# Two-engine halves for four PSUM copies, and a new pace for the background work, in a convolution, attention and mixture-of-experts kernel

## The chip, the core and the metric

The kernel runs on one core of one Trainium2 chip. A core has TensorE (PE in the profile; its weight loads are PEld), VectorE (DVE), ScalarE (ACT), GpSimd (POOL) and SyncE (SP, which here only issues DMAs). The metric is device time of the whole program in microseconds (us); lower is better. All data are float32.

## The reference, cut to what matters

```python
x = conv_attention(x)                 # (2, 256, 56, 56): 8 groups, linear attention, folded to one 256x256 map, + x, relu
t = to_tokens(x)                      # (2, 3136, 256)
n = layer_norm(t)
q, k, v = split(n @ W_attn)           # 4 heads of 64
t = t + softmax(causal(q k^T / 8)) v @ W_proj
n = layer_norm(t)
top2 of softmax(n @ gate_w + gate_b)  # 8 experts
t = t + sum over the two of weight * (gelu(n @ W1[e] + b1[e]) @ W2[e] + b2[e])
```

## The kernel before

**Stages.** In the profiled execution the convolution layer fills the first 94 us, attention of the two batches runs from 94 to about 865 us, and the experts with the sums at the end take the rest. The change touches `layer1`, which holds attention and experts.

**Attention.** A batch has 3136 tokens in 25 tiles of 128. Queries go in seven segments (`i` from 0 to 6) of W = 448 columns, heads in two pairs (`hp`). For each (i, hp), `attend` walks over the key tiles up to the diagonal: one *step* per key tile j. A step is `scores` (eight TensorE instructions of L660 into PSUM, then exp on ScalarE, L668; on the diagonal the causal mask on VectorE, L670; then the running sum of the exponentials on VectorE, L682, or L678 for the first) and, three steps later, `values` (L700). Key tiles that the diagonal cuts are interleaved with whole ones. Score tiles have two PSUM buffers (`psc`), exponentials five SBUF buffers.

**Visits.** When the steps of an (i, hp) are issued, `visit(i, hp)` is called, and then `sum_rows`, four small matmuls (`sp`, L724) of the running sum, copied out by ScalarE (L729). A visit prepares the next segment with *pieces* from `project_qkv`: at hp = 0 four Q/K projections (`query_key`, L540, copied out at L548), at hp = 1 one V projection for each of the next segment's token tiles (`value`, L557, copied out at L566, then L577 on VectorE), and at both a group of transposes of normalised rows (`transpose`, L526, copied to `px` at L532; GpSimd normalises, L511). The segments that are projected are 512 wide, the last two 384 and 192 (four V tiles, then three, then two). At i = 6 of the first batch the pieces are those of the second batch's first segments; at i = 6 of the second there are none. Each piece writes one PSUM bank of the pool `pm`, which has **two** buffers; products of the background, row sums, gate and sorting matmuls use the same two.

**Background work.** Generators stand in `queue`. `pull(n)` takes n items from them: a generator yields True after a piece of work, False when it can't go on, and "pe" when its next work is a matmul group; then it is *held* until `products()` in a visit lets it run (or a pull with `every`, in the experts' stage). `tokens(b)` runs in order: `project_gate` (batch 0; wt, wg), `project_out` (for pairs of tiles: matmuls `pp` L610, VectorE addition L615, then variances with `stats`, L168 and L169), `dispatch` (some 80 small VectorE operations that compute softmax, top two and slots, in `op`, `small_piece` and `apart` pauses; then 25 rows, each normalised on VectorE at L1294 and written by two indirect DMAs of GpSimd at L1302), the loads of w1 (SyncE) and the first expert rows. Batch 0's list runs during batch 1's attention, batch 1's in the experts' stage, where `meanwhile` pulls two or three items with `every` for each block of 128 rows. `between` is called before each step: on every second step it pulls two items. `visit` pulls twice as well.

**Order.** Attention and experts stand under a manual schedule: each engine executes in the order in which the program issues. An instruction that waits holds up all that stands behind it on its engine.

The lines around which the change turns:

```python
def visit(i, hp):
    now, then = ahead(b, i, hp)
    for piece in now:
        piece()
    for _ in range(2):
        pull()
        products()
    for piece in then:
        piece()
```

Of the kernel before, what the change touches and what calls it, by code (L numbers as in the profile page):

```python
# [28 lines left out]
def conv_attn_moe_kernel(  # L29
# [419 lines left out]
    def layer1(nm, general):  # L449

        with ExitStack() as whole:
# [45 lines left out]
            def project_qkv(b, qT, kT, v, px):  # L497

                def tiles(s):
                    return s[0] // P, -(-s[1] // P)  # L500

                todo = deque(p for s in SEGS for p in pairs(*tiles(s)))
                ready = {}

                def normalise():
                    if not todo:
                        return
                    n, m, k = todo.popleft()
                    xn = bg.tile([P, 2, C], F32, tag="xn", name=f"xn_{nm}{b}_{n}")
                    for a in range(m):  # L510
                        nc.gpsimd.tensor_scalar(  # L511
                            xn[:k, a], ts[b][:k, n + a, :C],
                            ts[b][:k, n + a, MEAN : MEAN + 1], ts[b][:k, n + a, RSTD : RSTD + 1],
                            ALU.subtract, ALU.mult,
                        )
                    ready[n] = xn

                def transpose(s, n, m, k):
                    if not ready:
                        normalise()  # L520
                    xn = ready.pop(n)
                    normalise()
                    tp = bank(f"xp_{b}_{n}", (P, NH, 2 * P))
                    for a in range(m):
                        for c in range(NH):
                            nc.tensor.transpose(  # L526
                                tp[:, c, a * P : a * P + k],
                                xn[:k, a, c * P : (c + 1) * P],
                                ident[:k, :k],
                            )  # L530
                    o, wp = n * P - SEGS[s][0], (m - 1) * P + k
                    nc.scalar.copy(px[:, s % 2, :, o : o + wp], tp[:, :, :wp])  # L532

                def query_key(s, which, hp):
                    first, end = SEGS[s]
                    w = end - first
                    ps = bank(f"qk_{b}_{s}_{which}_{hp}")
                    d0 = which * C + hp * P
                    for c in range(NH):
                        nc.tensor.matmul(  # L540
                            ps[:, :w],
                            wat[:, c, d0 : d0 + P],
                            px[:, s % 2, c, :w],
                            start=(c == 0),
                            stop=(c == NH - 1),
                        )
                    to = kT[hp] if which else qT[:, hp]
                    nc.scalar.copy(to[:, first:end], ps[:, :w])  # L548

                def value(s, n):  # L550
                    if b == 0 and n == 0:
                        centre_gate()
                    k = chunk(n)
                    ps = bank(f"v_{b}_{n}", (P, 512))
                    o = n * P - SEGS[s][0]
                    for c in range(NH):
                        nc.tensor.matmul(  # L557
                            ps[:k, : C + E],
                            px[:, s % 2, c, o : o + k],
                            wv[:, c].rearrange("p h d -> p (h d)"),  # L560
                            start=(c == 0),
                            stop=(c == NH - 1),
                        )
                    half = (C + E) // NH
                    for hp in range(NH):
                        nc.scalar.copy(  # L566
                            v[hp][:k, n].rearrange("p a d -> p (a d)"),
                            ps[:k, hp * half : (hp + 1) * half],
                        )
                    first, end = tiles(SEGS[s])  # L570
                    if n + 1 < end:
                        return
                    full = [n for n in range(first, end) if chunk(n) == P]
                    for f, e, k in ((first, first + len(full), P), (first + len(full), end, chunk(end - 1))):
                        for hp in range(NH if f < e else 0):
                            c0 = C + 2 * hp * LH
                            nc.vector.tensor_tensor(  # L577
                                ts[b][:k, f:e, c0 : c0 + 2 * LH].rearrange("p n (a e) -> p n a e", a=2),
                                v[hp][:k, f:e, :, HS:],
                                ts[b][:k, f:e, SLOT : SLOT + 1].unsqueeze(3).to_broadcast(  # L580
                                    [k, e - f, 2, LH]
                                ),
                                ALU.mult,
                            )
                    read[b] = end == NCH

                def xs(s):
                    return [partial(transpose, s, *p) for p in pairs(*tiles(SEGS[s]))] if s < NS else []

                def qks(s):  # L590
                    return [partial(query_key, s, which, hp) for which in range(2) for hp in range(NH)]

                def vs(s):
                    return [partial(value, s, n) for n in range(*tiles(SEGS[s]))]

                return xs, qks, vs
# [3 lines left out]
            def project_out(b, qT, done):  # L600

                for first, m, k in pairs():
# [3 lines left out]
                    for n in range(first, first + m):  # L606
# [8 lines left out]
                        nc.vector.tensor_tensor(t, t, ps[:k, : C + E], ALU.add)  # L615
                        if b == 0:
                            nc.sync.dma_start(out=rest_d[:k, n], in_=t[:, :C])
                    stats(b, first, m, k, bg, f"o{nm}{b}")

                    for _ in range(3 if b else 1):  # L620
                        yield True

            def attend(
                b, qT, kT, v, fst, fs, psc, py, visit, between, clock, later, finished
# [145 lines left out]
                for n in range(len(steps) + LAG):  # L770
# [3 lines left out]
                        sum_rows(hp, i)  # L774
                    if n < len(steps):
                        i = steps[n][0]
                        between(i, ends[i] - n)

                    late = n >= LAG and steps[n - LAG][3]
                    if n >= LAG:  # L780
# [162 lines left out]
            def dispatch(b):  # L943

                t = ts[b]
                tail = chunk(NCH - 1)
                ops = [0]

                def small_piece():

# [7 lines left out]

                def op():

                    ops[0] += 1
                    for _ in range(0 if b else 1 + ops[0] % 2):
                        yield True

                def small(name, last=E, dt=F32):
# [2 lines left out]
                def wide(ap):  # L968
# [8 lines left out]
                    small(k, 1).rearrange("p t o -> p (t o)") for k in ("newton_x", "newton_y", "red")  # L977
                )
                nc.vector.tensor_scalar(x, var, 1e-5, None, ALU.add)
                nc.vector.tensor_scalar(  # L980
                    y.bitcast(I32), x.bitcast(I32), 1, None, ALU.arith_shift_right
                )
                nc.vector.tensor_scalar(
                    y.bitcast(I32), y.bitcast(I32), -1.0, float(0x5F3759DF), ALU.mult, ALU.add
                )
                yield from small_piece()
                for i in range(4):
                    to = var if i == 3 else y
                    nc.vector.tensor_tensor(z, y, y, ALU.mult)
                    nc.vector.tensor_tensor(z, z, x, ALU.mult)  # L990
                    nc.vector.tensor_scalar(z, z, -0.5, 1.5, ALU.mult, ALU.add)
                    nc.vector.tensor_tensor(to, y, z, ALU.mult)
                    yield from op()
                    yield from small_piece()
# [294 lines left out]
                for n in range(NCH):  # L1289
# [23 lines left out]
                        if b or k:  # L1313
                            yield True
                    if b == 0:
                        yield False
                sent[b] = True

            def experts(w1s, w2s, b2s, ex, es, ps6, between, need, written):
# [327 lines left out]
            def pull(n=1, every=False):  # L1647

                while n > 0:
                    for g in list(queue):  # L1650
                        if g in held and not every:
                            continue
                        r = advance(g)
                        while r == "pe" and every:
                            r = advance(g)
                        if r is None or r is True:
                            n -= r is True
                            break
                    else:
                        return  # L1660
# [89 lines left out]
            else:  # L1750
# [26 lines left out]
                for b in range(B):  # L1777
                    queue.append(tokens(b, qT, lambda b=b: min(finished[b])))

                    def visit(i, hp):  # L1780

                        now, then = ahead(b, i, hp)
                        for piece in now:
                            piece()
                        for _ in range(2):
                            pull()
                            products()
                        for piece in then:
                            piece()

                    def between(i, left):
                        if b == B - 1 and i == NB - 1:

                            now = load_w2(left < NCH - 4)
# [1 line left out]
                                next(now, None)  # L1796

                        tick[0] += 1
                        if tick[0] % 2:
                            pull(2)  # L1800

                    due = attend(
                        b, qT, kT, v, fst, fs, psc, py, visit, between,
# [237 lines left out]
```

## Time and profile before

| | us |
|---|---|
| median of 16 runs (1297.36 to 1302.03) | 1299.76 |
| the profiled execution | 1300.63 |
| its span, first to last instruction | 1298.9 |
| TensorE busy in the span | 1251.7 |
| VectorE busy | 791.6 |
| ScalarE busy | 610.6 |
| mean granted TensorE clock | 0.993 |

A line of the timeline has the start (us from the span's start), the length of a run of like instructions, engine, line, operation, written tile and read tiles, the shape, the count, and in brackets the engine's idle time just before it with what ended it. A line of the waits has the waiting instruction, what released it, the total in us, how often, and the longest. Running instructions can overlap on TensorE, so that a run's length may reach past the start of the next.

### The profile page before, as it was taken

The page shows a single profiled execution, that of the slowest core. Times are in us where ns is not written, and L with a number is a line of the kernel's source. Part 1 is how long each engine was busy: PE and PEld are TensorE (multiplying, and loading weights), DVE is VectorE, ACT ScalarE, POOL GpSimd, SP SyncE. Part 2 cuts the span into 40 slices and gives each one's busy share as a digit, 9 for nine tenths or more (in the row PEclk, how much of TensorE's full clock was granted, in tenths as well). Part 3 has the DMA queues.
Part 4 walks back from the last instruction along what each step waited for, and adds up shares of the span by engine and source line. Part 5 has one row for each costly group of instructions (what it writes and reads, how often), then busy time and mean ns, then how long its engine had stood idle before and what let it go on. Part 6 is the DMA issues. An engine that isn't in the chain of part 4 may idle for free.

```text
span 1298.9 us, 28049 instructions
## 1 busy us (share of the span) xinstructions
PE 1251.7 (96%) x10569; PEld 821.9 (63%) x10569; DVE 791.6 (61%) x1659; ACT 610.6 (47%) x1228; POOL 350.9 (27%) x317
## 2 busy tenths in 40 slices
PE   7998999999999999999999999999999999999994
PEld 7874445444444454534444444469899899989993
DVE  1482557676677764668687877755675443455552
ACT  0144555465656555356555655552433333444441
POOL 1102412110002204221115760000047312675641
PEclk9999999999999999999999999999999999999997
DMA  9995011000000000100001243231135443576553
GB/s 294 383 304 179 16 24 33 25 9 25 9 17 9 26 1 11 39 9 16 9 9 61 93 162 103 71 100 53 54 126 169 127 114 95 153 226 204 180 162 103
DMA packets 110655, 123.55 MB, mean 95 GB/s; under 512 B 20019, under 2 KB 100260, under 8 KB 110512
## 3 DMA queue, kind: packets, MB, share of 16 engines
q1 hardware_dynamic: 97104, 93.12, 23.9%
q0 software_dynamic: 9984, 25.76, 5.9%
q10 hardware_dynamic: 3424, 2.78, 0.7%
q8 instruction: 87, 1.43, 0.5%
q14 instruction: 56, 0.46, 0.1%
HBM read 62.65 MB, written 60.41 MB: 95 GB/s over the span
## 4 chain that ended last, share of the span: by engine, by line
PE 79%; DVE 6%; DMA 5%; issue 4%; ACT 2%; POOL 2%; POOLq 0%; DVEq 0%; ACTq 0%; SPq 0%
PE yp_f L700 17%; PE sc_f L660 16%; PE ht_f L1421 13%; PE yp_f L1440 12%; PE qk_f L540 6%; PE cp L330 3%; PE v_f L557 3%; DVE acc_f L682 3%; PE gram L261 2%; PE pp_f L610 2%; POOL x_slots L1302 2%; ACT st_f L668 2%; PE tp_f L1398 2%; DMA y_tokens<-ys_f,to_f 1%; DMA kept<-t 1%
## 5 line engine op out<-in xcount | busy, mean ns | idle before, releaser
L668 ACT ACTIVATE st_f<-sc_f 128x896 f32<-128x896 f32 (+5 forms) x400 | 331.0, 840 | 215.1 <-PE sc_f L660 197.7
L682 DVE TENSOR_TENSOR acc_f<-acc_f,st_f 128x896 f32<-128x896 f32 (+5 forms) x372 | 379.6, 1020 | 67.6 <-ACT st_f L668 56.3
L700 PE MATMUL yp_f<-st_f,v_f 64*64 64x448 f32 (+6 forms) x3184 | 339.8, 501 | 4.6 <-DVE st_f L670 3.5
L660 PE MATMUL sc_f<-qT_f,kT_f 64*64 64x448 f32 (+6 forms) x3184 | 339.7, 499 | 3.3 <-ACT st_f L668 2.1
L1430 ACT ACTIVATE g_f<-ht_f,b1b 128x128 f32<-128x128 f32 x408 | 116.3, 368 | 222.6 <-PE ht_f L1421 222.5
L660 PEld LDWEIGHTS sc_f<-qT_f,kT_f 64*64 64x64 f32 x3184 | 122.5, 133 | 154.3 <-issue 124.7
L700 PEld LDWEIGHTS yp_f<-st_f,v_f 64*64 64x64 f32 x3184 | 119.8, 133 | 155.6 <-issue 131.3
L1421 PE MATMUL ht_f<-xT_f,w_f 128*128 128x128 f32 x1632 | 199.4, 275 | 0.8 <-ACT xT_f L1402 0.8
L1421 PEld LDWEIGHTS ht_f<-xT_f,w_f 128*128 128x128 f32 x1632 | 196.1, 192 | 5.6 <-ACT xT_f L1402 1.0
L712 POOL TENSOR_TENSOR qT_f<-both_f 128x448 f32<-128x448 f32 x28 | 37.0, 1322 | 488.7 <-ACT both_f L711 488.6
L1302 POOL DMA_INDIRECT x_slots<-xr_f,idx x100 | 111.8, 1118 | 127.7 <-DVE xr_f L1300 90.6
L511 POOL TENSOR_SCALAR xn_f<-t 128x256 f32<-128x256 f32 (+1 forms) x50 | 80.2, 1611 | 172.0 <-PE xp_f L526 66.2
L1409 DVE COPY w_f<-w1s_f 128x1024 f32 x102 | 71.1, 698 | 54.4 <-PE ht_f L1421 52.8
L1457 POOL DMA_INDIRECT y_tokens<-ys_f,to_f x60 | 61.8, 1030 | 121.8 <-DVE ys_f L1450 96.4
L1450 DVE TENSOR_TENSOR ys_f<-yp_f,kT_f 128x128 f32<-128x128 f32 x102 | 29.6, 290 | 101.9 <-PE yp_f L1440 97.5
L540 PE MATMUL qk_f<-px_f,wat 128*128 128x512 f32 (+2 forms) x224 | 88.1, 546 | 1.2 <-ACT px_f L532 1.2
L540 PEld LDWEIGHTS qk_f<-px_f,wat 128*128 128x128 f32 x224 | 40.6, 190 | 46.9 <-issue 41.6
L670 DVE TENSOR_TENSOR st_f<-st_f,keep 128x256 f32<-128x256 f32 (+1 forms) x112 | 45.4, 405 | 32.8 <-ACT st_f L668 32.8
L678 DVE COPY acc_f<-st_f 128x896 f32<-128x896 f32 x28 | 17.7, 633 | 77.1 <-ACT st_f L668 76.8
L1440 PE MATMUL yp_f<-px_f,g_f 128*128 x204 | 61.4, 383 | 0.0
L1440 PE MATMUL yp_f<-v_f,g_f 128*128 x204 | 61.1, 382 | 0.0
L1440 PE MATMUL yp_f<-kT_f,g_f 128*128 x204 | 61.1, 382 | 0.0
(255 smaller groups left out, 1254.3 us busy)
## 6 DMA issues: line engine op xcount, KB each, us to landing
x_slots<-fill SPq DMA_DIRECT2D x1, 8127.0 KB
xb_f<-x_slots SPq DMA_DIRECT2D x60, 129.0 KB
x_slots<-fill SPq DMA_DIRECT2D x1, 7296.0 KB
y_slots<-ys_f SPq DMA_DIRECT2D x57, 128.0 KB
kept<-t SPq DMA_DIRECT2D x2, 3200.0 KB
x<-in_x_dram SPq DMA_DIRECT2D x14, 448.0 KB
rb_f<-inverses SPq DMA_DIRECT2D x56, 112.0 KB
xr<-in_x_rows_dram SPq DMA_DIRECT2D x12, 512.0 KB
```

The source lines that it names most:

```text
L511: nc.gpsimd.tensor_scalar(xn[:k, a], ts[b][:k, n + a, :C], ts[b][:k, n + a, MEAN : MEAN + 1], ts[b][:k, n + a, RSTD : RSTD + 1], ALU.subtr ...
L540: nc.tensor.matmul(ps[:, :w], wat[:, c, d0 : d0 + P], px[:, s % 2, c, :w], start=(c == 0), stop=(c == NH - 1),)
L660: nc.tensor.matmul(ps[h : h + HS, a, c0:W], kT[hp][rows, j * P + h : j * P + h + HS], qT[rows, hp, q0 + c0 : q0 + W], start=True, stop=True,)
L668: nc.scalar.activation(st[:k, :, c0:], ps[:k, :, c0:W], AF.Exp, scale=SCALE)
L682: nc.vector.tensor_tensor(acc[:k, :, c0:], acc[:k, :, c0:], st[:k, :, c0:], ALU.add)
L700: nc.tensor.matmul(yp[a * HS : (a + 1) * HS, h // HS, c0:W], v[hp][h : h + HS, j, a, :HS], st[h : h + HS, a, c0:], start=first, stop=bool( ...
L1302: s = nc.gpsimd.indirect_dma_start(out=xds[b], out_offset=bass.IndirectOffsetOnAxis(ap=idxs[b][:kk, k, n : n + 1], axis=0), in_=xr[:kk], i ...
L1409: nc.vector.tensor_copy(w, w1s[:, :, bass.ds(e, 1), :].rearrange("p c e h -> p c (e h)"))
L1421: nc.tensor.matmul(ht[:, k, :], w[:, c, k * P : (k + 1) * P], xT[:, c, :], start=(c == 0), stop=(c == NH - 1),)
L1430: nc.scalar.activation(g[:, k, :], ht[:, k, :], AF.Gelu, bias=b1bs[b][:, k, i : i + 1])
L1440: nc.tensor.matmul(yp[:, :C], g[:, k, :], w2s[k][:, bass.ds(e, 1), :].rearrange("p e d -> p (e d)"), start=(k == 0), stop=(k == KH - 1),)
L1457: s = nc.gpsimd.indirect_dma_start(out=y_tokens, out_offset=bass.IndirectOffsetOnAxis(ap=to[:, n % GB : n % GB + 1], axis=0), in_=ys, in_o ...
```

## The change

Four parts:

- `leave` copies a projection's result out of PSUM in two halves: the first by ScalarE, the second by VectorE. Transposed rows are halved by the two row groups of 128 channels, Q and K by columns, V by head pair. Until now ScalarE made the whole copy (for V, two copies).
- A visit issues all its pieces, transposes included, and then the background's products. It pulls nothing any more.
- The variances of projected tiles become generators of their own (`closer`), put at the front of the queue, one tile an item. `dispatch` gives up one operation an item in batch 0, the Newton steps included; a scattered row takes two items.
- `between` pulls one item at every step, but none at the cut steps of the first segment. A pull with `every` lets a generator go past at most one "pe" and counts the next one as an item.

```diff
--- before.py
+++ after.py
@@ -499,6 +499,11 @@
                 def tiles(s):
                     return s[0] // P, -(-s[1] // P)
 
+                def leave(first, second):
+
+                    nc.scalar.copy(*first)
+                    nc.vector.tensor_copy(*second)
+
                 todo = deque(p for s in SEGS for p in pairs(*tiles(s)))
                 ready = {}
 
@@ -529,7 +534,7 @@
                                 ident[:k, :k],
                             )
                     o, wp = n * P - SEGS[s][0], (m - 1) * P + k
-                    nc.scalar.copy(px[:, s % 2, :, o : o + wp], tp[:, :, :wp])
+                    leave(*((px[:, s % 2, c, o : o + wp], tp[:, c, :wp]) for c in range(NH)))
 
                 def query_key(s, which, hp):
                     first, end = SEGS[s]
@@ -545,7 +550,7 @@
                             stop=(c == NH - 1),
                         )
                     to = kT[hp] if which else qT[:, hp]
-                    nc.scalar.copy(to[:, first:end], ps[:, :w])
+                    leave(*((to[:, first + c : first + c + w // 2], ps[:, c : c + w // 2]) for c in (0, w // 2)))
 
                 def value(s, n):
                     if b == 0 and n == 0:
@@ -562,11 +567,12 @@
                             stop=(c == NH - 1),
                         )
                     half = (C + E) // NH
-                    for hp in range(NH):
-                        nc.scalar.copy(
-                            v[hp][:k, n].rearrange("p a d -> p (a d)"),
-                            ps[:k, hp * half : (hp + 1) * half],
-                        )
+                    leave(
+                        *(
+                            (v[hp][:k, n].rearrange("p a d -> p (a d)"), ps[:k, hp * half : (hp + 1) * half])
+                            for hp in range(NH)
+                        )
+                    )
                     first, end = tiles(SEGS[s])
                     if n + 1 < end:
                         return
@@ -615,10 +621,18 @@
                         nc.vector.tensor_tensor(t, t, ps[:k, : C + E], ALU.add)
                         if b == 0:
                             nc.sync.dma_start(out=rest_d[:k, n], in_=t[:, :C])
-                    stats(b, first, m, k, bg, f"o{nm}{b}")
-
-                    for _ in range(3 if b else 1):
-                        yield True
+                    queue.appendleft(closer(b, first, m, k))
+                while unclosed[b]:
+                    yield False
+
+            unclosed = [NCH] * B
+
+            def closer(b, first, m, k):
+
+                for n in range(first, first + m):
+                    stats(b, n, 1, k, bg, f"o{nm}{b}")
+                    unclosed[b] -= 1
+                    yield True
 
             def attend(
                 b, qT, kT, v, fst, fs, psc, py, visit, between, clock, later, finished
@@ -774,7 +788,7 @@
                         sum_rows(hp, i)
                     if n < len(steps):
                         i = steps[n][0]
-                        between(i, ends[i] - n)
+                        between(i, ends[i] - n, (steps[n][2] + 1) * P > i * W + 1)
 
                     late = n >= LAG and steps[n - LAG][3]
                     if n >= LAG:
@@ -944,7 +958,6 @@
 
                 t = ts[b]
                 tail = chunk(NCH - 1)
-                ops = [0]
 
                 def small_piece():
 
@@ -958,8 +971,7 @@
 
                 def op():
 
-                    ops[0] += 1
-                    for _ in range(0 if b else 1 + ops[0] % 2):
+                    if b == 0:
                         yield True
 
                 def small(name, last=E, dt=F32):
@@ -977,18 +989,24 @@
                     small(k, 1).rearrange("p t o -> p (t o)") for k in ("newton_x", "newton_y", "red")
                 )
                 nc.vector.tensor_scalar(x, var, 1e-5, None, ALU.add)
+                yield from op()
                 nc.vector.tensor_scalar(
                     y.bitcast(I32), x.bitcast(I32), 1, None, ALU.arith_shift_right
                 )
+                yield from op()
                 nc.vector.tensor_scalar(
                     y.bitcast(I32), y.bitcast(I32), -1.0, float(0x5F3759DF), ALU.mult, ALU.add
                 )
+                yield from op()
                 yield from small_piece()
                 for i in range(4):
                     to = var if i == 3 else y
                     nc.vector.tensor_tensor(z, y, y, ALU.mult)
+                    yield from op()
                     nc.vector.tensor_tensor(z, z, x, ALU.mult)
+                    yield from op()
                     nc.vector.tensor_scalar(z, z, -0.5, 1.5, ALU.mult, ALU.add)
+                    yield from op()
                     nc.vector.tensor_tensor(to, y, z, ALU.mult)
                     yield from op()
                     yield from small_piece()
@@ -1313,7 +1331,7 @@
                         if b or k:
                             yield True
                     if b == 0:
-                        yield False
+                        yield True
                 sent[b] = True
 
             def experts(w1s, w2s, b2s, ex, es, ps6, between, need, written):
@@ -1651,8 +1669,9 @@
                         if g in held and not every:
                             continue
                         r = advance(g)
-                        while r == "pe" and every:
+                        if r == "pe" and every:
                             r = advance(g)
+                            r = True if r == "pe" else r
                         if r is None or r is True:
                             n -= r is True
                             break
@@ -1780,15 +1799,12 @@
                     def visit(i, hp):
 
                         now, then = ahead(b, i, hp)
-                        for piece in now:
+                        for piece in now + then:
                             piece()
                         for _ in range(2):
-                            pull()
                             products()
-                        for piece in then:
-                            piece()
-
-                    def between(i, left):
+
+                    def between(i, left, cut):
                         if b == B - 1 and i == NB - 1:
 
                             now = load_w2(left < NCH - 4)
@@ -1796,8 +1812,8 @@
                                 next(now, None)
 
                         tick[0] += 1
-                        if tick[0] % 2:
-                            pull(2)
+                        if not cut or i:
+                            pull()
 
                     due = attend(
                         b, qT, kT, v, fst, fs, psc, py, visit, between,
```

## Prediction

> **What bounds the kernel now.** I read the page first (busy shares and chain), then TensorE's list of waits over the attention stage (94 to 870 us), then the timeline around two visits, then the groups by shape for the price of each copy.
>
> ```profile
> PE 1251.7 (96%) x10569; PEld 821.9 (63%) x10569; DVE 791.6 (61%) x1659; ACT 610.6 (47%) x1228; POOL 350.9 (27%) x317
> PE 79%; DVE 6%; DMA 5%; issue 4%; ACT 2%; POOL 2%; POOLq 0%; DVEq 0%; ACTq 0%; SPq 0%
> ```
>
> TensorE is busy for 1251.7 of 1298.9 us. The change leaves its matmuls as they are, so it can only move the 47 us between them, and every new wait of TensorE is paid in full. What it can win stands in TensorE's waits of the attention stage (us in total, times, longest):
>
> ```profile
> PE yp_f L700 <- DVE st_f L670: 3.5, 7, 1.0
> PE xp_f L526 <- DVE t L615: 2.2, 6, 1.1
> ...
> PE sp_f L724 <- DVE t L615: 1.9, 3, 0.7
> PE sp_f L724 <- ACT kT_f L548: 1.5, 6, 0.4
> PE qk_f L540 <- ACT px_f L532: 1.2, 1, 1.2
> ...
> PE sp_f L724 <- ACT v_f L566: 0.9, 3, 0.3
> ...
> PE wg_f L490 <- ACT wT_f L484: 0.7, 1, 0.7
> ```
>
> The whole list is 17 us. 3.5 of it is the causal mask coming late behind other VectorE work; 7.7 stands at visits (xp and pp behind L615, 2.2 and 0.6; sp behind L615, kT, v, px and L577: 1.9, 1.5, 0.9, 0.4, 0.2), where transposes, projections and row sums share two PSUM buffers. So the prize is about 10 us. The price is read from the timeline of a V visit, the one at 263.9 us:
>
> ```profile
> 263.90 3.83 PE L557 MATMUL v_f<-wv,px_f 128*128 128x264 f32 x16
> ...
> 264.09 0.92 ACT L668 ACTIVATE st_f<-sc_f 128x896 f32<-128x896 f32 x1 [0.85 <-PE sc_f L660]
> 264.51 1.62 DVE L682 TENSOR_TENSOR acc_f<-acc_f,st_f 128x256 f32<-128x256 f32 x2
> 265.10 0.44 ACT L566 COPY v_f<-v_f 128x132 f32<-128x132 f32 x2
> ...
> 268.26 0.59 PE L724 MATMUL sp_f<-acc_f,ones 128*32 128x224 f32 x8 [0.31 <-ACT v_f L566]
> ```
>
> and of the end of a Q/K visit:
>
> ```profile
> 150.31 0.60 PE L526 MATMUL xp_f<-ident,xn_f 128*128 128x128 f32 x4
> ...
> 150.50 0.58 ACT L548 COPY kT_f<-qk_f 128x512 f32<-128x512 f32 x1 [1.13 <-PE qk_f L540]
> ...
> 151.14 0.59 PE L724 MATMUL sp_f<-acc_f,ones 128*32 128x224 f32 x8 [0.24 <-ACT kT_f L548]
> ```
>
> In the first the reader is to see that ScalarE is free for the first V tile at 265.0, while VectorE works until 266.13 on the last running sum, 2.2 us after the visit began. In the second, one copy of 0.58 decides when the row sums start.
>
> **The change, part by part.**
>
> *1. Copies in halves.* In the built program each VectorE half waits for a count of ScalarE's semaphore that rises by one with each copy, while ScalarE's half waits for TensorE: the halves of one bank go one after the other. And the third tile of a run waits for VectorE. So an eviction becomes: hand-over 0.05, ScalarE half, hand-over 0.03, VectorE half, hand-over 0.04. Rows: ScalarE 128x256 takes 0.384 (L532), 128x132 0.272 (L566). VectorE out of PSUM alone: 128x257 0.428 (L269); for 128x132 the nearest row is L1450, 128x128 with a second operand, 0.28. A Q/K tile now needs 0.05 + 0.586 + 0.04 = 0.68 us, afterwards 0.05 + 0.384 + 0.03 + 0.43 + 0.04 = 0.93. A V tile's two copies take 0.44, 0.53 with hand-overs; afterwards 0.05 + 0.27 + 0.03 + 0.28 + 0.04 = 0.67. For VectorE's V half the bounds are 0.13 (its smallest row, a 1x1) and 0.43; I take 0.28, the nearest width.
>
> The order at a visit is now pieces, transposes, products, sums. Priced by visit (i from 0 to 6, two batches):
> - Q/K visits: 12. Whoever uses the bank of the fourth tile (sp, or pp where there are products) waits 0.24 + 0.25 = 0.49. Eight are full width (3.9), two 384 wide (0.45 each), two 192 wide (0.2 each): 5.2.
> - V visits, third tile: i = 1 to 4. TensorE wants it 2 x 0.89 = 1.78 after the start; VectorE is free at 2.23, plus 0.28 and 0.04 is 2.55: 0.77 each, 3.1 in the first batch. In the second, sorting pieces lie ahead: at 591.64 and 645.99 VectorE is free 3.23 and 2.72 after the start (1.8 and 1.3 of wait). With one piece a step there is less ahead: 0.77, 0.77, 1.2, 0.9: 3.6.
> - V visits, last tile: the wait of sp is 0.09 or 0.31 now, by the width of the transposes beside it, and 0.14 longer afterwards: 10 x 0.3 = 3.0.
> - V visits with two tiles (i = 5): sp takes the first tile's bank and waits as the third tile does: 2 x 0.77 = 1.5.
> - i = 6: in batch 0 two transposes (1.14) go ahead of the products, whose bank leaves at 2.23 + 0.43 + 0.04 = 2.70: 1.5; the next visit 0.4. In batch 1 four products stand alone; the third waits for an addition (0.42) behind the last sum: 2.66 - 1.78 = 0.88, twice. Together 3.7.
>
> Sum 20.0 in place of 7.7: **+12.3**. At the start, before the first scores: the first Q/K piece waits for two px copies, the second half 0.67 later; the gate's L469 now queues behind VectorE's kT half, 104.20 becomes 104.70; ScalarE's last px copy is 0.2 shorter: **+1.0**. VectorE's added 48 us of copies (56 of about 0.42, 26 of 0.42, 50 of 0.28) lie beside TensorE's work except where named.
>
> The Trainium skill, "PSUM — Partial Sum Buffer", section "PSUM bank collisions raise a hardware error", says that ScalarE and VectorE may not read one bank in the same partitions at the same time. No run here shows such a collision; the built order agrees with the rule. Side by side, a Q/K eviction would be an estimated 0.05 + 0.43 + 0.04 = 0.52, and the Q/K visits 0.16 shorter each, not 0.25 longer.
>
> *2. Pieces one a step.* Variances (0.41 + 0.18 a tile, L168 and L169) become single pieces taken at following steps; sorting gives one operation a step, not two pulls every second step. Work is the same. The 3.5 us of late masks all stand after 550 us, where bursts such as L989 to L992 (0.30 + 0.19 + 0.19 + 0.19) run ahead of a mask. These small ones go; the 0.36 to 0.84 ones stay, and on the diagonal a pair of steps has 2.24 of VectorE work (0.45 + 0.7 + 1.09) before any piece against 2.35 on TensorE. Bounds: -3.5, and +3.5 (as many late masks again); I take **-2.0**, nearer the burst's row.
>
> *3. Gate projection* moves to the visits of i = 1: its 0.7 wait has a whole visit for cover, but sp then waits for px, 0.93 against 0.60 of transposes: **-0.4**.
>
> *4. Later work.* In program order the scatter of batch 0 starts nine steps later and ends in the last step of i = 5; w1's eight loads and the first rows are still issued before the last segment's row sums, some 40 us ahead of use: nothing, and if that cover went, 4 MB of loads would stand in front of the experts. Batch 1's scatter starts later by three small operations (0.9), and its second tile by one expert block. POOL runs its 50 indirect DMAs back to back, 1.28 us each, from 955.8 to 1023.0, and the expert transposes at 1031.1 wait 2.7 for what it wrote. Bounds 0 and one tile (2.6); I take the middle, **+1.3**. The order behind that is the same.
>
> Sum: 12.3 + 1.0 - 2.0 - 0.4 + 1.3 = +12.2 on the profiled execution's 1300.6 us, 1312.8; that run is 0.9 above the median of 1299.8, so **1312**.
>
> **Rivals.**
> - *Faster: the halves are hidden and the thinner queue pays.* Place: the third V tile and the first user after a visit. It decides if VectorE's last sum ends within 1.4 us of the visit's start (now 2.2): then no copy is waited for. Gone are 7.7 at visits, 3.5 of masks, 0.7 of gate; 1.0 and 1.3 remain: -9.6, about 1290. For: the page has VectorE at 61%. Against: 0.92 of exp and 1.09 of sum follow the last scores whatever the pieces do.
> - *A wash*: VectorE's halves cost at the bounds below (third tiles 0.6, Q/K 0.3, no longer tails, i = 6 2.5: 14 against 7.7), masks -3.5, the start 0.5, no delay of the scatter: +2.6 or less; about 1301.
> - *VectorE becomes the bound in batch 1*: all third tiles there wait 1.8 (+3.5), masks come later (+5.5 against my term), the scatter a full tile (+1.3), and a third more for the tails: about 1325. For: up to nine tenths busy in the page's slices already at 715 to 780 us (52.97 of 65).
> - *The halves run side by side after all*: the V halves still queue behind the sum; only the 12 Q/K visits win 0.41 each: about 1307, inside my range.
>
> **How the numbers follow.** Forecast 0.76 (that includes the last rival), wash 0.09, faster 0.08, VectorE-bound 0.07. My terms at their bounds give 1302 to 1321; the range 1302 to 1320 leaves out the faster rival, half the wash and most of the VectorE case. Within 0.2% (2.6 us, about what a measurement of this kernel can tell from no change) lies most of the wash and a corner of the forecast: 0.10; faster 0.08; slower 0.82.
>
> **What would show it.** Right: in TensorE's waits, V matmuls waiting for a VectorE copy of V, eight times, 0.8 to 1.2 each; sp and pp waiting for VectorE copies of kT and v; late masks at about 1.5 us; the expert transposes waiting near 4 us; TensorE's busy time unchanged. Wrong: no V matmul waits; the VectorE half starts with the ScalarE half; mask waits grow past 3.5.

## The result, and the profile after

The changed kernel takes **1327.82 us** (median of 8 runs, 1326.53 to 1332.8) against 1299.14 (median of 44): a ratio of **1.0227, 95% interval 1.0217 to 1.0236**. It is slower by 28.7 us; the forecast was 12 slower, with a range that ended at 1320. In the profiled executions the span goes from 1298.9 to 1328.2 us, by 29.3.

The busy line of the page, as at the start of the prediction:

```profile
PE 1261.4 (95%) x10569; PEld 820.6 (62%) x10569; DVE 830.2 (63%) x1793; ACT 588.0 (44%) x1178; POOL 354.3 (27%) x317
```

The matmuls are the same 10569, yet TensorE is busy 9.7 us longer: some of them became slower, and some wait inside what counts as busy. VectorE has 38.6 more, by the halves. The list of TensorE's waits in the attention stage (94 to 890 us), which was 17 us long and now is 32.1:

```profile
PE v_f L562 <- DVE v_f L505: 7.9, 10, 1.4
PE sp_f L738 <- DVE v_f L505: 5.4, 9, 2.9
PE qk_f L545 <- DVE qT_f L505: 3.6, 3, 2.3
PE sp_f L738 <- DVE kT_f L505: 2.5, 5, 0.6
PE pp_f L616 <- DVE kT_f L505: 2.0, 4, 0.6
...
PE pp_f L616 <- DVE px_f L505: 1.6, 1, 1.6
...
PE yp_f L714 <- DVE st_f L684: 0.3, 1, 0.3
```

L505 is VectorE's half. All of TensorE's waits for it, with three small ones that are not shown (0.5, 0.3, 0.2), are 24.0 us. The late mask (last line) went from 3.5 to 0.3. The V visit that the prediction showed at 263.9 now begins at 268.8; its timeline:

```profile
268.80 2.05 PE L562 MATMUL v_f<-wv,px_f 128*128 128x264 f32 x8
...
269.40 1.62 DVE L696 TENSOR_TENSOR acc_f<-acc_f,st_f 128x256 f32<-128x256 f32 x2
269.99 0.27 ACT L504 COPY v_f<-v_f 128x132 f32<-128x132 f32 x1
...
270.94 0.54 DVE L505 COPY v_f<-v_f 128x132 f32<-128x132 f32 x2
...
271.29 2.05 PE L562 MATMUL v_f<-wv,px_f 128*128 128x264 f32 x8 [0.44 <-DVE v_f L505]
```

ScalarE's half is over at 270.26. VectorE adds the last running sum until 271.0, and only then copies; TensorE, through with two tiles, stands until a bank is free. The bracket shows 0.44 of it, since TensorE's ends are modelled: by the distance of the two starts, 2.49, against 1.78 for two tiles, it is 0.7. That is the wait that was forecast at 0.77. The rest of it counts as busy time of the V matmuls, as their groups show, before and after (count, busy time in us, mean in ns, idle time ahead and what ended it):

```profile
L557 PE MATMUL v_f<-wv,px_f 128*128 128x264 f32 (+1 forms) x200 | 48.5, 393 | 0.6 <-DVE gwc L469 0.6
L562 PE MATMUL v_f<-wv,px_f 128*128 128x264 f32 (+1 forms) x200 | 51.5, 400 | 8.8 <-DVE v_f L505 7.9 <-DVE gwc L469 0.9
```

So 3.0 of the 9.7 are these waits under another name; no V matmul ran at a lowered clock. What was not forecast is the Q/K visit of i = 5 in batch 1:

```profile
757.02 0.41 DVE L1312 TENSOR_SCALAR xr_f<-t 128x256 f32<-128x256 f32 x1 [1.06 <-DMA x_slots<-xr_f,idx]
757.35 1.08 DVE L696 TENSOR_TENSOR acc_f<-acc_f,st_f 128x896 f32<-128x896 f32 x1
...
759.14 0.41 DVE L1312 TENSOR_SCALAR xr_f<-t 128x256 f32<-128x256 f32 x1
759.46 1.08 DVE L696 TENSOR_TENSOR acc_f<-acc_f,st_f 128x896 f32<-128x896 f32 x1
760.47 0.41 DVE L505 COPY qT_f<-qk_f 128x96 f32<-128x96 f32 x2
...
760.77 2.20 PE L545 MATMUL qk_f<-px_f,wat 128*128 128x192 f32 x8 [2.27 <-DVE qT_f L505]
```

At 755.96 VectorE wants to write a scatter row (L1312) into one of two buffers and waits 1.06 for the indirect DMA that still reads it. Sums, mask and a second row queue up behind, and the half of the first Q tile, ready at 758.2, is copied at 760.47. At the same visit of batch 0, where there are no rows, TensorE waits 0.88 for the last sums alone (at 371.74), so the rows and the DMA make the other 1.4. The wait for the DMA is old. VectorE's waits at this line, 640 to 890 us, in the kernel before:

```profile
DVE xr_f L1294 <- DMA x_slots<-xr_f,idx: 6.6, 7, 1.8
```

and in the changed one:

```profile
DVE xr_f L1312 <- DMA x_slots<-xr_f,idx: 4.1, 4, 1.9
```

It used to be longer in total, and cost TensorE less, though not nothing. Behind three of the rows that waited, TensorE waited in its turn: for a mask at 705.44 (0.49) and at 744.22 (0.38), and here for an addition:

```profile
750.22 0.41 DVE L1294 TENSOR_SCALAR xr_f<-t 128x256 f32<-128x256 f32 x1 [1.19 <-DMA x_slots<-xr_f,idx]
...
751.02 0.59 PE L724 MATMUL sp_f<-acc_f,ones 128*32 128x224 f32 x8 [0.72 <-DVE t L615]
```

How much of the new waits is the DMA's own, two executions of the changed kernel tell (the second is the repeat on another chip, further down). At the V visit of i = 5 in batch 1, the first has

```profile
796.62 0.41 DVE L1312 TENSOR_SCALAR xr_f<-t 128x256 f32<-128x256 f32 x1 [1.95 <-DMA x_slots<-xr_f,idx]
...
799.28 0.98 PE L738 MATMUL sp_f<-acc_f,ones 128*32 128x224 f32 x8 [2.92 <-DVE v_f L505]
```

and the second

```profile
793.62 0.41 DVE L1312 TENSOR_SCALAR xr_f<-t 128x256 f32<-128x256 f32 x1
...
796.28 0.59 PE L738 MATMUL sp_f<-acc_f,ones 128*32 128x224 f32 x8 [0.95 <-DVE v_f L505]
```

There the wait for the DMA is passed on in full: 1.95 less at the row, 1.97 less on TensorE. At the Q/K visit it is the smaller part: with 0.45 at the row in place of 1.06, TensorE still waits 1.92 in place of 2.27.

The last line of the Q/K visit's timeline has a second thing in it: its eight matmuls take 2.20; the eight before them, of the same shape, took 1.57. The same stretch in windows of 2 us (columns: window, length, busy time of PE, PEld, DVE, ACT and POOL with instructions, granted TensorE clock, DMA share, GB/s):

```profile
760.00:762.00 2.00, 1.23 (x6) 1.23 (x7) 0.88 (x3) 0.24 (x1) 1.70 (x2) 0.89 0.13 47
762.00:764.00 2.00, 2.00 (x16) 0.86 (x18) 0.52 (x2) 0.29 (x2) 1.65 (x2) 0.50 0.34 119
764.00:766.00 2.00, 2.00 (x20) 0.73 (x21) 0.00 (x0) 0.29 (x1) 0.00 (x0) 0.76 0.19 67
```

After the idle time the granted clock is 0.50 for 3.4 us, and work of 1.7 takes 3.4. This happens four times in the changed kernel (at 761, 799, 901 and 1062 us, after waits of 2.27, 2.92, 3.45 and 4.03), and once in the kernel before (at 1031, after 2.68), the last sums of either left aside. Three times 1.7 is an estimated 5.1 of the 9.7. The other new waits are in the experts' stage (890 us to the end):

```profile
PE tp_f L1416 <- issue: 4.0, 1, 4.0
PE pp_f L616 <- DVE t L621: 3.4, 1, 3.4
PE rank_f L1079 <- DVE both_f L1068: 1.6, 1, 1.6
```

They were 2.7, nothing and 0.5.

### The profile page after: what moved, and what is told of

The parts are those of the page before. It is cut to its first block, busy times and chain, and to the rows that moved or that the text cites. A ratio compares the mean times of both kernels' runs of the same rounds, so it can differ in the third digit from the quotient of the medians.

```text
span 1328.2 us, 28056 instructions
## 1 busy us (share of the span) xinstructions
PE 1261.4 (95%) x10569; PEld 820.6 (62%) x10569; DVE 830.2 (63%) x1793; ACT 588.0 (44%) x1178; POOL 354.3 (27%) x317
## 4 chain that ended last, share of the span: by engine, by line
PE 65%; issue 18%; POOL 6%; DMA 5%; DVE 4%; ACT 2%; POOLq 0%; DVEq 0%; SPq 0%; ACTq 0%
PE ht_f L1439 13%; PE yp_f L714 12%; PE yp_f L1458 12%; PE sc_f L674 12%; PE qk_f L545 3%; PE pp_f L616 3%; PE gram L261 3%; POOL x_slots L1320 3%; POOL xn_f L516 2%; DMA kept<-t 2%; PE cp L330 2%; PE tp_f L1416 2%; DVE acc_f L696 1%; PE v_f L562 1%; ACT st_f L682 1%
## 5 line engine op out<-in xcount | busy, mean ns | idle before, releaser
L1458 PE MATMUL yp_f<-w2s_f,g_f 128*128 x204 | 61.1, 382 | 0.0
L1532 POOL DMA_INDIRECT y_f<-y_slots,idx x50 | 55.9, 1119 | 18.9 <-issue 18.6
```

The costliest lines, as they stand in the source:

```text
L1458: nc.tensor.matmul(yp[:, :C], g[:, k, :], w2s[k][:, bass.ds(e, 1), :].rearrange("p e d -> p (e d)"), start=(k == 0), stop=(k == KH - 1),)
```

## The experiments

The experiments ran on four chips, of two sorts: on two of them ("faster") the kernel before takes 1297 to 1298 us, on two ("slower") 1332 to 1337. The slower ones show more waits of TensorE for instruction issue (14.9 us against 4.8 in the one variant that ran on both, V whole); what makes up the rest stays open. A ratio is always against the kernel before on the same chip. **Theory 1**: VectorE's halves stand in an in-order queue, and TensorE waits for what stands ahead of them. **Theory 2**: the new pacing costs the time. **Theory 3**: the order of pieces, transposes and products in a visit does. **Theory 4**: the new lines of `pull` cost in the experts' stage.

**All copies whole on ScalarE**, the rest as changed:

```diff
-leave(*((px[:, s % 2, c, o : o + wp], tp[:, c, :wp]) for c in range(NH)))
+nc.scalar.copy(px[:, s % 2, :, o : o + wp], tp[:, :, :wp])
```

and so for Q, K and (two copies) V.

> All of the change, but every tile of transposes, Q, K and V leaves PSUM on ScalarE alone, as in the kernel before (one copy for transposes, Q and K, two for V). Theory 1 (the second half queues in VectorE behind row sums and behind scatter rows that wait for a DMA, so TensorE waits at visits): the visits lose 17 to 22 us of their excess, about 1304 to 1311, and the two visits at 757 and 797 us shrink by 3 us each. Theory 2 (the loss comes from the new pacing: one operation a step, closers, a later scatter): 1320 to 1328. Theory 3 (the loss comes from transposes and pieces standing ahead of the products): 1320 to 1328 as well, with sp and pp still waiting at visits, now for ScalarE.

1304.18 us, ratio 1.0040 (1.0026 to 1.0053): 23.6 of the 28.7 are the halves. TensorE's waits for these copies are now for ScalarE; the longest of them, 94 to 890 us:

```profile
PE sp_f L737 <- ACT kT_f L553: 1.3, 5, 0.3
PE qk_f L545 <- ACT px_f L537: 1.2, 1, 1.2
PE sp_f L737 <- ACT v_f L571: 1.2, 4, 0.3
PE pp_f L615 <- ACT kT_f L553: 1.1, 4, 0.4
```

With 0.5 and 0.2 more, 5.5 in place of 24.0: 18.5 less. TensorE's busy time is 6.9 less (1254.5). Together 25.4, and the spans differ by 24.8 (1328.2 to 1303.4). Theory 1 holds; by 2 or 3 the time would have stayed where it was.

**The halves alone**, in the kernel before:

> The kernel before with the copies in halves and nothing else of the change. Theory 1 (the halves are the cost): at least as far from 1299 as the halves' share of the change, 1315 to 1322. Theories 2 and 3 (pacing or the order of the visit): 1299 to 1305. If the halves cost clearly less here than whole copies win in the changed kernel, then it is the two together, halves behind an order that asks for them sooner.

1319.01 us, 1.0156 (1.0136 to 1.0175), 20.8 more, in the range of theory 1. The first expert block starts 22.9 later than in the kernel before (889.1 against 866.2) with the same work done; part of that comes back in the experts' stage, where the transposes wait 2.1 for the scatter, not 2.7. So the halves need no help from the new order to cost what they do.

**The old inner loop of pull:**

```diff
-if r == "pe" and every:
-    r = advance(g)
-    r = True if r == "pe" else r
+while r == "pe" and every:
+    r = advance(g)
```

> The changed kernel with the old inner loop of pull, which goes on only while the generator hands back products. Theory 4 (in the experts' stage the new lines advance a held generator twice, so that four products stand in a row on two banks at 901 us, 3.4 of wait and 1.7 at half the clock): the wait of pp for L621 in that stage is gone and the time is about 1322 to 1324. If the four products are not from these lines: 1327 to 1329, with the wait still there.

1320.08 us, 1.0175 (1.0152 to 1.0198): some 7 less, more than expected, and by another way. The two longest of TensorE's waits, 885 to 1100 us:

```profile
PE pp_f L616 <- DVE t L621: 3.2, 1, 3.2
PE rank_f L1079 <- DVE both_f L1068: 1.9, 1, 1.9
```

The wait of the products is still there; the one that went is tp's 4.0, and the half clock behind it. The order of TensorE's work tells why. With the old loop all fifteen product tiles that are left for this stage stand in one row, and one pull is spent on them; with the new lines they stand in rows of four, four, four and three, at four pulls. The rank matmuls then come in the 18th block, not the 17th, and the scatter of batch 1 starts in the 23rd, not the 22nd. A block takes 3.7, and tp waits 4.0 for what the scatter wrote. The kernel before has its rank matmuls in the 18th block too, so the new lines do not delay the sort against it: the old loop, without the yields, brings it forward. Theory 4 had the right lines and the wrong mechanism.

**Whole copies and the old loop:**

> Whole copies on ScalarE and the old inner loop of pull; the rest is the changed kernel: the new order in a visit, variances as closers, one operation a step. Theories 1 and 4 together: both shares add, 1298 to 1306, beside or below the kernel before, with late masks still gone. Theories 2 or 3: 1315 and above.

1298.77 us, 1.0003 (0.9993 to 1.0013), level with the kernel before. Halves and pull together are the whole loss; new order, closers and one operation a step are worth nothing measurable between them. That is a balance and not an absence: 3.2 of late masks and the 2.7 of tp are gone, 2.8 at the products and 1.4 at rank are new.

**Both halves on ScalarE:**

```diff
-nc.vector.tensor_copy(*second)
+nc.scalar.copy(*second)
```

> The changed kernel with both halves copied by ScalarE: the same number of copies and the same two-step hand-over, but nothing stands in VectorE's queue. Theory 1 (the queue in VectorE is the cost): 1304 to 1309, next to whole copies, the rest being a second fixed cost of some 0.2 for each copy. Rival (the cost is the cut itself, two short copies one after the other): 1317 to 1328.

1.0033 (1.0009 to 1.0058; 1338.83 on a slower chip), beside the whole copies' 1.0040 on a faster one. The changed kernel did not run on that chip, but 0.3% is far from its 2.3%. Cutting an eviction in two costs next to nothing by itself; the queue on VectorE is the cost.

**V whole, and Q, K and transposes whole.** On a slower chip first:

> The changed kernel with only the V tiles whole again on ScalarE (two copies); transposes, Q and K stay in halves. If the queue behind VectorE's row sums at V visits is the larger share of the 24 us that whole copies won in the changed kernel: V's share is 13 to 15, about 1313 to 1315, and v matmuls no longer wait for a VectorE copy. If Q, K and the transposes are the larger share: 1316 to 1322.

> The changed kernel with transposes, Q and K whole on ScalarE and only the V tiles in halves. The run with V whole gave 1.0094 of the kernel before, against 1.0227 with all halves and 1.004 with none, so V's halves looked like 1.3% (17 us) and the others like 0.5%. If the shares add: 1.017 to 1.019 here, about 1321 to 1323. If they overlap (the late V copy and the late Q copy stand behind the same VectorE work): closer to 1.013.

1.0094 (1.006 to 1.0128) and 1.0131 (1.0086 to 1.0175); the changed kernel did not run beside them, and the intervals are wide. So all three on one faster chip:

> The changed kernel as it is, as the mark for the three runs beside it on the same chip. The earlier comparison gave 1.0227. If the chip has no part in it: 1.021 to 1.024.

> The changed kernel with V whole on ScalarE, again, now beside the changed kernel. If V's halves are the larger share of the 24 us: 12 to 17 us less than the changed kernel on this chip. If Q, K and the transposes are: 7 to 12 less.

> The changed kernel with transposes, Q and K whole, V in halves, again, beside the changed kernel. If the shares of the two parts add to the 24 us that whole copies won: 7 to 12 less than the changed kernel, the rest of what V whole leaves. If they overlap: the two gains sum to clearly more than 24.

The changed kernel 1327.28 (1.0237, 1.0215 to 1.026), V whole 1312.12 (1.0116, 1.0099 to 1.0133), Q, K and transposes whole 1317.23 (1.0155, 1.0138 to 1.0172). The halves of V cost 15.2, the others 10.1. They sum to 25.3, near the 23.6 of all: the shares add, as far as four runs each can tell (those of the changed kernel go from 1323.69 to 1329.66).

**The row ahead of the halves.** First on GpSimd, which issues the scatter itself:

```diff
-nc.vector.tensor_scalar(
+nc.gpsimd.tensor_scalar(
     xr[:kk, :C], t[:kk, n, :C],
```

> The changed kernel with the scatter rows of L1312 computed on GpSimd, which issues the scatter itself, so that VectorE never waits there for the DMA that reads the row buffer. Theory 1 in its second part (the two visits of i = 5 in batch 1 cost 3.3 and 3.9 because VectorE's copy stood behind L1312, and each brought some 1.7 of half clock): both waits of 2.3 and 2.9 go, about 1320 to 1323. If that wait came from VectorE's work and not from the DMA: 1326 to 1329, with both waits still there.

1.0367 (1.0333 to 1.0401), much slower, though the two waits did shrink: the longest wait of sp for v fell from 2.9 to 0.5, of qk for qT from 2.3 to 1.2. The edit moves the rows of both batches. GpSimd needs a mean of 1.46 for a row (median 1.27), the scatter came late, and TensorE waited 38.1 for it at 1108 us (and 13.3 for an exp at 836, which was not followed up). The second try leaves the row on VectorE and gives the DMA a step more:

```diff
 if b == 0:
     yield True
+    yield True
```

> The changed kernel with one more step between the scatter rows of batch 0, so that the DMA that reads a row buffer is done before VectorE wants the buffer again. All arithmetic stays in its place; the scatter ends some 25 steps later. Theory 1, second part: VectorE's waits at L1312 for that DMA (4.1 in total, longest 1.9) go, and with them the waits of 2.3 for qT and 2.9 for v and the half clock behind each, 5 to 8 less than the changed kernel: 1319 to 1323. If the scatter is then late for the first expert rows: no gain or a loss, and a wait ahead of the first experts shows it.

> The changed kernel with one more step between scatter rows of batch 0, again, beside the changed kernel. If VectorE's waits for the DMA of the row buffer cost TensorE the 2.3 and 2.9 and the half clock behind them: 4 to 9 less than the changed kernel. If the later scatter gives it back in the experts' stage: 0 to 3 less.

On a slower chip 1.0162 (1.012 to 1.0204); beside the changed kernel 1335.4 us, 1.0293 (1.0275 to 1.031), 8 slower than it. In both, VectorE's waits at L1312 are gone from its list, and the waits of sp for v and of qk for qT are at most 0.4 and 0.9. But no row stands among the last sums of the two visits any more either, so these runs price rows and DMA together; the DMA alone shows in the two executions above. And a wait is new: sp for the last sum at the first visit of i = 6, 3.3 and 2.2. In the second, the later scatter held back the sorting of batch 1 (rank in the 21st block, not the 18th), and TensorE paid for that in the experts' stage:

```profile
PE tp_f L1417 <- DVE xb_f L1394: 14.8, 1, 14.8
```

That the waits go with the rows is shown three times, a net gain never. More row buffers, which might take the wait for the DMA away and move nothing else, were not tried.

**The old order in a visit**, with whole copies:

> Whole copies on ScalarE, and in a visit the old order of pieces, products, transposes; the pacing and the pull of the changed kernel stay. It stands beside the whole-copy run with the new order (1.004). Theory 3 (the order itself costs or wins): differs from 1.004 by over 0.2%. Theories 1 and 2: 1.002 to 1.006, and the 7.7 of waits of xp, pp and sp behind L615 at visits come back in part while others go.

1.0018 (0.9992 to 1.0044) on a slower chip, against 1.0040 (1.0026 to 1.0053) on a faster one: not told apart.

**The products in a row.** One yield after each pair of batch 1, with whole copies and the old loop:

```diff
 queue.appendleft(closer(b, first, m, k))
+if b:
+    yield True
```

> Whole copies, the old inner loop of pull, and in batch 1 one more yield after each pair of output projections (the kernel before had three). In the experts' stage the whole-copy runs still show four products in a row on two banks: TensorE waits 2.8 for L620 at 873 us and runs at half clock behind it. If the yields that the change takes out are the cause: that wait goes, 1293 to 1296, some 3 to 5 below the run without the yield, and below the kernel before by 0.2 to 0.4%. If the products stand in a row for another reason: 1298 to 1300.

1.011 (1.0079 to 1.0141), a miss. The wait of 2.8 is gone, but the yields also spend pulls during attention: nineteen tiles are left for the experts' stage, not fifteen, the rank matmuls come in the 22nd block, and the transposes wait 3.9 for the scatter. With the yield after one pair only (`if b and first == 10`):

> Whole copies and the old loop of pull, as in the run that stood level with the kernel before (1.0003), and one yield after the first pair of output projections that falls into the experts' stage. There all 15 tiles of products stood in one row, and the third waited 2.8 for VectorE, with half a clock behind it. Now two stand alone, and thirteen follow a block later, when VectorE is through. If that is what the wait is: 3 to 5 less, 0.996 to 0.998 of the kernel before. If VectorE is late there again: 1.000.

> Whole copies, the old loop of pull, one yield after the first pair in the experts' stage, the new order in a visit; again. If the wait of the third product tile (2.8) and the half clock behind it are what the yield takes away: 0.996 to 0.998 of the kernel before, 1292 to 1296. If the gain was the slower chip's: 0.999 to 1.001.

> The same with the old order in a visit: pieces, products, transposes. Theory 3 (the order matters by itself): differs from the run beside it by 3 or more, since the transposes' waits behind L620 come back (2.2 in the kernel before) and those of pp for kT and px (1.6) go. Otherwise: within 2 of it.

0.9972 (0.995 to 0.9994), again 0.9981 (0.9964 to 0.9998), and with the old order 0.9988 (0.9968 to 1.0009), all on the slower chips, the last two on the same one. The longest wait of the products for VectorE is 0.6 in all three, so the yields that the change takes out were the cause of that wait. The first two are one kernel, the only one here whose interval lies below both kernels, by 0.2 to 0.3%; no faster chip ran it. The order makes a difference of 0.0007, which is within the noise; nothing of theory 3 is seen.

## Why the prediction was right in sign and wrong in size

| term (us, profiled executions) | predicted | measured |
|---|---|---|
| TensorE's waits in attention, without masks | +12.9 (12.3 + 1.0 - 0.4) | +17.8 |
| the part of them that counts as busy time of the V matmuls | in the line above | +3.0 |
| late masks | -2.0 | -3.2 |
| transposes behind the scatter | +1.3 | +1.3 |
| products and rank in the experts' stage | 0 | +4.5 (3.4 + 1.1) |
| TensorE at half clock | 0 | +5.1 (3 x 1.7, worked out) |
| sum | 12.2 | 28.5 of 29.3 |

The remaining 0.8 is assigned to nothing.

**Right.** TensorE is the bound, and no new wait is hidden. ScalarE's half first, VectorE's half after it, the third V tile waiting for VectorE's running sum (0.77 forecast, 0.7 at 271.3), sp and pp waiting for halves of kT and v, transposes waiting 4.0 ("near 4"), masks no longer late. The rival of halves side by side is out: in all 134 pairs of the changed kernel's trace VectorE's half starts after ScalarE's ends. The wash and the faster rival fail as they said they would, by what stands ahead of the copy.

**Wrong, step 1.** "VectorE is free at 2.23" took only the sum as standing ahead. The Q/K and the V visit of i = 5 in batch 1 found scatter rows ahead, and a wait for a DMA with them: 2.3 and 2.9, where 0.2 and 0.77 were priced. Even without rows the narrow Q/K visit costs 0.88, since two tiles 192 wide are done before the last sums are. And third V tiles were counted for i = 1 to 4, at 6.7; the list has ten such waits, i = 0 among them, by the distances of the starts 0.7 to 1.7 each and 10.6 together. The two make 4.2 and 3.9, about the 7.9 (4.9 and 3.0) by which the term is short; smaller misses cancel. The trace of before had the rows' waits for the DMA (6.6), and two of the late masks that the prediction put down to bursts of sorting (705.44 and 744.22) stand behind such rows.

**Wrong, step 4.** "The order behind that is the same" did not follow the change into the experts' stage. It takes out the three yields after each pair of batch 1, so that products stand in rows on two banks, with either inner loop, and wait 2.5 to 3.4 for VectorE where they waited for nothing; rank waits 1.1 longer. That is the 4.5 that was put at nothing. The new lines of `pull` are a second matter: the runs put 5.4 (1304.18 to 1298.77, with whole copies) to 7 on them against the old loop, which would bring the sort a block forward; against the kernel before they leave the sort in its block.

**Wrong, the first sentence.** That "every new wait of TensorE is paid in full" is too low: a wait above some 2 us can cost 1.7 on top, for the half clock behind it. "TensorE's busy time unchanged", given as the sign of a right forecast, is what failed most plainly: 1251.7 to 1261.4, an estimated 5.1 of it by the clock. The row that would have told was in the trace of before: at 1031.09 TensorE had waited 2.68, and from 1032 to 1034 the granted clock was 0.50.

**The rival that came nearest in time** was VectorE as the bound in batch 1, about 1325. That is luck: its steps did not happen. Third tiles there wait 0.8 to 1.7 by their starts, not 1.8 each, masks come earlier, not later, and the scatter is 1.3 late, not a tile. The range ended at 1320 since two terms, the experts' stage and the clock, were costed at nothing and had no bound of their own.

The Trainium skill, "TensorE: Matmul & The Clock Gate", section "What's actually happening", says that the clock is halved after at least one idle window of about 3.4 us and full again after as long a busy one, and that the windows run freely. The 3.4 us at 0.50 agree with that; the idle time ahead of it was shorter here, 2.07 to 2.92 in seven cases, and the measurement decides.

## What to carry to other kernels

Moving a copy to an engine with spare time moves it into that engine's queue: price it by the time at which the last instruction ahead of it can end, waits for DMAs included, not by the engine's busy share. A DMA wait that costs little on an engine off the path becomes TensorE's wait as soon as TensorE needs anything behind it. Where work is paced by pulls, count the pulls that each piece takes up to the thing that is waited for last.

## What the runs showed of the hardware that was not expected

- **Half clock after short idles.** In ten traces of the faster sort (the kernel before, two of the changed one, and seven variants), each idle of TensorE of 3.1 us or more before the final sums was followed by a granted clock of 0.50. Of those between 2.0 and 3.0 some were (2.07, 2.21, 2.27, 2.68, 2.82, 2.90, 2.92) and some were not (2.06, 2.54, 2.73, 2.97); of those below 2.0, none. The slower chips' traces do not keep to this: two idles there (3.35 and 3.41) were not followed by a drop, and drops came with no idle of 2.0 just ahead, six of them in the first run with the old order in a visit.
- **One kernel, several times.** Two profiled executions of the changed kernel had four such drops (3.4 each) and one (6.8), and spans of 1328.2 and 1322.0. An estimated 3.4 of the 6.2 is the clock, and 2.3 is what the waits for the row's DMA made of the two visits of i = 5.
- **Chips can differ more than kernels.** The kernel before took 1298.24 on one chip and 1332.54 on another. Ratios taken on different chips are no safe ground for sums: the parts came to 1.3% and 1.0% that way for what is 1.9% in all, though with intervals that wide (0.7 and 0.9%) this may be noise.
